# The second sequence's scan: GpSimd adds the two states of every second step, and the planner counts one sum product there

## The chip, the cores and the metric

The kernel runs on one core of a Trainium2 chip. The core has TensorE (PE in the profile; PEld is its weight load), VectorE (DVE), ScalarE (ACT), GpSimd (POOL) and SyncE (SP), which here only issues transfers. The metric is device time in microseconds. Three runs of the kernel before gave 990.7, 991.05 and 991.42 us; the median is 991.05.

## The reference, cut to what matters

The kernel computes a small network of four layers over two sequences (`b` = 0, 1) of 512 positions and 512 features, each with a normalized residual:

```python
x = x + ln(mamba(ln(x)))       # L0_attn: 1024 channels, 16 states a channel
x = x + ln(gptq_ffn(ln(x)))    # L0_ffn: 4-bit weights, 512 -> 1376 -> 512
x = x + ln(attention(ln(x)))   # L1_attn
x = x + ln(latent_moe(ln(x)))  # L1_ffn
```

The change is in the first layer, a selective scan. For every channel d, with 16 states n:

```python
def step(state, inp):                       # over the 512 positions
    dt_t, B_t, C_t, u_t = inp
    dA = exp(dt_t[..., None] * A)
    state = state * dA + (dt_t * u_t)[..., None] * B_t[:, None, :]
    y = einsum('bdn,bn->bd', state, C_t)    # the sum over the 16 states
    return state, y
y = y + u * D
y = y * silu(gate)
out = y @ W_out.T
```

The second layer unpacks 4-bit weights for gate, up and down, and computes `(gate * sigmoid(gate) * up) @ Wd`.

## The kernel before, in words

Everything is float32 with 128 rows (partitions) by 512 columns as the usual tile. In the scan a tile holds 128 channels by 512 positions; a sequence has 8 such channel blocks (`NCH`), so there are 16 blocks in the list `order`: first the 8 of sequence 0, then the 8 of sequence 1. The 16 states of a block are worked two at a time (`NG` = 2), so a block takes 8 steps (`NGI` = 8) and the whole scan 128 (`s` = 0 to 127). Step s belongs to block k = s // 8 and is its step gi = s % 8. Blocks of sequence 1 are steps 64 to 127.

What one step does, engine by engine:

- ScalarE writes exp(dt * A) for the two states into PSUM (`exps`, L970).
- VectorE multiplies `du` (dt times u, in PSUM) by the two rows of B into a `bx` tile of 128 x 2 x 512 (`times_B`, L986), then runs the recurrence over it in place (`scan`, L990). `bx` has six buffers (L625).
- GpSimd multiplies the tile by C in place (`times_C`, L996).
- TensorE adds the states up: `sums` (L998 to L1010) multiplies each of the two halves with the identity and accumulates in the PSUM tile `y`, which has one bank. The block's first sum has one more product in front of it, with the diagonal of D (L1004). A float32 product of 128 x 512 stands in the profile as two records.
- When a block's 16 states are in, `fin` (L1012, its instruction is L1015) multiplies `y` into the gate on VectorE.

A Python loop over s (from L1031 on) writes the instructions out in order, and `pin()` fixes that order for TensorE, ScalarE, VectorE and GpSimd; SyncE's queue is not pinned. Within an iteration s stand: `fin` of the block before (at gi == 2), TensorE's part, `times_B(s + 1)`, `scan(s)`, `exps(s + 2)`, `times_C(s)`. TensorE's part has two halves: the sums of step s - 2, and a stream of other work, `stream()` (L928). A budget decides how much of the stream goes into a step: every step adds `STEP` = 3.5 us, every product takes `MM` = 0.86 us off (L677, L678), sums included, and the stream is drawn from while the budget is above zero. At gi == 2 the stream stands ahead of the sums, else behind them.

The stream is a chain of generators: gates and input products of both sequences, then the output products of sequence 0 (`out_tiles`, L876, with weights `wo` through L834; it waits for `fin` of block 7), the transposes of its normalized rows, and last `ffn0()` (L910): 11 column groups, each with four `fg` and four `fu` products (L919). Each product group spawns a job, run by `tick()` twice an iteration: for a gate, three ScalarE instructions (L656 to L658) and a GpSimd product (L660, `it<-ti,it`); for an up, a VectorE product from PSUM (`ffn_up_job`, L907, `it<-it,fu`). `out_job` copies or reads an output row tile, normalizes it with statistics on VectorE (L119 to L125), small GpSimd instructions (L127, L134), an application on ScalarE (L150), and a GpSimd add into x (L827). Two PSUM banks serve the whole stream, handed from one group to the next in turn (`bank`, `release`).

What the stream hasn't given when the loop ends is written out behind it (`for _ in pe`) and isn't pinned. Then comes stage p3: 32 output products of sequence 1 (`po`, L1092, weights `wo`), the unpacking of the down weights (`once`, L296: loads through L189, L212 and L220, nibbles L226, subtraction L309 on VectorE, product L310 on GpSimd, stores to memory L317 and L327), and 44 down products of sequence 0 (`fo`, L1114, whose weights `wd` are read back through L1109). Its tiles lie where the scan's `bx` tiles lay. The weight tiles `wg`, `wu`, `wo` and `wd` share three buffers of 512 KB (tag `w4`).

Of the kernel before, what the change touches and what calls it, by code (L numbers as in the profile page):

```python
# [29 lines left out]
N_ST = 16  # L30
# [4 lines left out]
NG = 2  # L35
NGI = N_ST // NG
# [20 lines left out]
def tile_sandwich(  # L57
# [5 lines left out]
    nc = tc.nc  # L63
# [24 lines left out]
    ident = const.tile([P, P], F32, name="ident")  # L88
# [299 lines left out]
    def pin():  # L388

        seen = nc.cur_bb.bb.instructions  # L390
        for ins in seen[behind.get("n", 0) :]:
            if ins.engine not in ORDERED:
                continue
            prev = behind.get(ins.engine)
            if prev is not None:
                tc.add_manual_dep(
                    ins, prev.name,
                    mybir.DependencyInfo(mybir.DependencyClass.NoSync, mybir.DependencyReason.DATA),
                    reason="order of tracing",
                )  # L400
            behind[ins.engine] = ins
        behind["n"] = len(seen)
# [6 lines left out]
    with ExitStack() as mamba:  # L409
# [35 lines left out]
        st = {}  # L445
# [21 lines left out]
        def diag(k):  # L467

            c = k % NCH
            t_ = dgp.tile([P, P], F32, tag="dg", name=f"dg{k}")  # L470
            nc.scalar.activation(t_, ident, AF.Copy, scale=ch[:, c, KCONV + 1 : KCONV + 2])
            st["diag", k] = t_
# [49 lines left out]
        def states(b, gi):  # L522

            for lst, lo, nm in ((Bbs[b], 0, "B"), (Cbs[b], R_C - R_B, "C")):
                t_ = bcp.tile([P, NG, S], F32, tag=f"{nm}{gi}", name=f"{nm}{b}_{gi}")
                n0 = lo + gi * NG
                ins = nc.sync.dma_start(
                    out=t_, in_=scr[b][n0 : n0 + NG, :].partition_broadcast(P)
                )
                lst[gi] = t_  # L530
            return ins

        def dt_in(b, c):
            ps = mbank(f"pv{b}_{c}")
            nc.tensor.matmul(ps, wdt[:, ts(c, P)], dtT[b], start=True, stop=True)
            return ps
# [9 lines left out]
        with ExitStack() as p1:  # L546
# [65 lines left out]
            for gi in range(NGI):  # L612
                last = states(0, gi)
# [10 lines left out]
        with ExitStack() as p2:  # L624
# [17 lines left out]
            def spawn(gen, lag=0):  # L642
                jobs.append([now[0] + lag, gen])

            def tick():
                now[0] += 1
                for job in list(jobs):
                    if job[0] <= now[0]:
                        try:
                            job[0] = now[0] + next(job[1])  # L650
                        except StopIteration:
                            jobs.remove(job)
# [12 lines left out]
            def bank_free():  # L665
                return len(turns) < 2 or turns[-2][1] is not None
# [10 lines left out]
            MM = 0.86  # L677
# [283 lines left out]
            order = [(b, c) for b in range(B) for c in range(NCH)]  # L961
            NS = len(order) * NGI
            bxs = {}

            def exps(s):
                k, gi = divmod(s, NGI)
                b, c = order[k]
                for i in range(NG):
                    n = gi * NG + i
                    nc.scalar.activation(  # L970
                        das[s % 2][:, i, 1:], st["dt", b, c][:, 1:], AF.Exp, scale=A[:, c, n : n + 1]
                    )

            def new_du(k):

                b, c = order[k]
                du = st["du"] = ps_du.tile([P, S], F32, tag="du", name=f"du{b}_{c}")
                nc.scalar.copy(du, st["dt", b, c])

            def times_B(s):  # L980
                k, gi = divmod(s, NGI)
                b, c = order[k]
                if gi == 0:
                    nc.vector.tensor_mul(st["du"], u[b][c], st["du"])
                bx = bxs[s] = bxp.tile([P, NG, S], F32, tag="bx", name=f"bx{b}_{c}_{gi}")
                nc.vector.tensor_mul(bx, st["du"].unsqueeze(1).to_broadcast([P, NG, S]), Bbs[b][gi])  # L986

            def scan(s):
                flat = bxs[s].rearrange("p n t -> p (n t)")
                nc.vector.tensor_tensor_scan(  # L990
                    flat, das[s % 2].rearrange("p n t -> p (n t)"), flat, 0.0, ALU.mult, ALU.add
                )

            def times_C(s):
                b, c = order[s // NGI]
                nc.gpsimd.tensor_mul(bxs[s], bxs[s], Cbs[b][s % NGI])  # L996

            def sums(s):  # L998
                k, gi = divmod(s, NGI)
                b, c = order[k]  # L1000
                cost = NG * MM
                if gi == 0:
                    y = st["y"] = ps_y.tile([P, S], F32, tag="y", name=f"py{b}_{c}")
                    nc.tensor.matmul(y, st["diag", k], u[b][c], start=True, stop=False)  # L1004
                    cost += MM
                bx = bxs.pop(s)
                for i in range(NG):
                    n = gi * NG + i
                    nc.tensor.matmul(st["y"], ident, bx[:, i, :], start=False, stop=(n == N_ST - 1))  # L1009
                return cost  # L1010

            def fin(k):  # L1012

                b, c = order[k]
                nc.vector.tensor_mul(g[b][c], g[b][c], st["y"])  # L1015
                st[f"fin{k}"] = now[0]

            def dt_job(k, ps):
                dt_out(*order[k], ps)
                release(f"pv{k}")  # L1020
                yield 1
# [9 lines left out]
            for s in range(NS + 3):  # L1031
                k, gi = divmod(s, NGI)
                free = min(free, MM) + STEP
                if gi == 1 and k + 1 < len(order):
                    dt_due = k + 1
                if gi == 2 and k:
                    fin(k - 1)
                for part in ((1, 0) if gi == 2 else (0, 1)):
                    if part == 0:
                        if 0 <= s - 2 < NS:  # L1040
                            free -= sums(s - 2)
                    else:
                        while free > 0 and s < NS:
                            if dt_due and bank_free():
                                turns.append([f"pv{dt_due}", None])
                                spawn(dt_job(dt_due, dt_in(*order[dt_due])), 2)
                                free -= MM
                                dt_due = None
                            cost = next(pe, None)
                            if cost is None:  # L1050
                                break
                            free -= cost
                tick()
                if gi == 4 and k + 1 < len(order):
                    diag(k + 1)
                if 0 < s < NS - 1:
                    times_B(s + 1)
                    if gi == NGI - 2 and k + 1 < len(order):
                        new_du(k + 1)
                tick()  # L1060
                if s < NS:
                    scan(s)
                    if s == 0:
                        times_B(1)
                    if s + 2 < NS:
                        exps(s + 2)
                    times_C(s)
                    if order[k] == (0, NCH - 1):
                        states(1, gi)
                pin()  # L1070
# [6 lines left out]
        with ExitStack() as p3:  # L1077
# [9 lines left out]
            for j in range(NCH // 2):  # L1087
                w = wo_pair(1, 0, j)
                for e in range(2):
                    c = 2 * j + e  # L1090
                    for i in range(TB):
                        nc.tensor.matmul(  # L1092
                            po[i], g[1][c][:, ts(i, P)], w[:, e, :],
                            start=(c == 0), stop=(c == NCH - 1),
# [9 lines left out]
            for i, m in enumerate(IC):  # L1104
                j, e = divmod(i, 2)
                if not e:
                    w = wst.tile([P, 2, H], F32, tag="w4", name=f"wd0_{j}")
                    n = len(IC[i : i + 2])
# [4 lines left out]
                for t in range(TB):  # L1113
                    nc.tensor.matmul(  # L1114
                        fo[t], its[i][:m, ts(t, P)], w[:m, e],
                        start=(i == 0), stop=(i == len(IC) - 1),
# [279 lines left out]
```

## Time and profile before

| what | us |
|---|---|
| median of three runs | 991.05 |
| the profiled execution, its own time | 991.02 |
| its span, first to last instruction | 989.0 |
| busy: PE, DVE, ACT, POOL | 878.8, 688.8, 426.0, 478.3 |
| first and last scan instruction start | 71.0, 596.0 |
| first `po`, first `fo`, last `fo` product start | 619.1, 646.9, 684.3 |

Times inside the profile count from the span's start. In rows of instruction groups stand the line, the engine, the operation, output and inputs, the shapes, the count, then the busy time, the mean of one in nanoseconds, and the idle time of that engine ahead of them with what ended most of it. In the stretch rows the columns are the stretch, its length, the busy time with the number of instructions for PE, PEld, DVE, ACT and POOL, the granted TensorE clock, the share of DMA time and GB/s. In rows of waits stand who waited, for whom, the time in all, how often, and the longest. In the chain stand start, length, and what ran; "issue" is time in which nothing that the profile shows was waited for, and SPq is SyncE's queue issuing a transfer.

### The profile page before, as it was taken

Reading aid. Unit: us, or ns where it says so; the run is one execution under the profiler, and the core shown is the slowest. Engines: PE = TensorE matmul, PEld = TensorE weight load, DVE = VectorE, ACT = ScalarE, POOL = GpSimd, SP = SyncE. Lnnn points to the kernel's source line nnn. Section 1 sums busy time; section 2 is a strip of 40 time slices with the busy share of each in tenths; the row PEclk is TensorE's granted clock in tenths of the full one; section 3 lists DMA queues with packets and bytes.
Section 4 is the critical chain, followed back from the end, with each engine's and each line's share of the span. In section 5 each row is a group of like instructions: output and inputs, shape, how many; then the busy total and the mean of one; then the engine's idle time right before and its main releaser. Section 6 shows DMA issues by size and latency. Waiting matters only on the chain.

```text
span 989.0 us, 7214 instructions
## 1 busy us (share of the span) xinstructions
PE 878.8 (89%) x2216; PEld 393.8 (40%) x2216; DVE 688.8 (70%) x775; ACT 426.0 (43%) x639; POOL 478.3 (48%) x351
## 2 busy tenths in 40 slices
PE   6966868778899989978999999999999998999994
PEld 3532323233353434423443343444544444455442
DVE  4846999999999998999998995553530014715225
ACT  4345645465666754567664642032430013421212
POOL 4645886787777876776766664450000000001002
PEclk9989998799999989999999999999999999999998
DMA  6358110110100673410100112454322231100101
GB/s 195 113 182 350 43 53 15 37 44 28 43 1 24 209 263 112 139 53 0 43 21 22 42 29 73 143 182 136 127 64 64 58 105 54 64 1 32 54 0 42
DMA packets 43608, 80.61 MB, mean 82 GB/s; under 512 B 7822, under 2 KB 20217, under 8 KB 43570
## 3 DMA queue, kind: packets, MB, share of 16 engines
q1 hardware_dynamic: 40786, 72.72, 22.3%
q0 software_dynamic: 2496, 6.92, 1.8%
q10 hardware_dynamic: 288, 0.52, 0.1%
q8 instruction: 17, 0.28, 0.1%
q14 instruction: 21, 0.17, 0.1%
HBM read 68.90 MB, written 11.24 MB: 81 GB/s over the span
## 4 chain that ended last, share of the span: by engine, by line
PE 39%; DVE 31%; issue 12%; POOL 7%; ACT 2%; DMA 2%; SPq 1%; DVEq 0%; POOLq 0%; ACTq 0%
DVE bx L990 11%; DVE bx L986 8%; PE py L1009 6%; PE pup L1261 5%; POOL bx L996 4%; PE fo L1114 4%; PE pd L1324 4%; PE fu L354 3%; PE fo L1177 3%; PE fg L354 3%; DVE q_gu L226 3%; PE fu L919 2%; PE fg L919 2%; DVE u L462 1%; PE pr L1292 1%
## 5 line engine op out<-in xcount | busy, mean ns | idle before, releaser
L996 POOL TENSOR_TENSOR bx<-bx,C 128x1024 f32<-128x1024 f32 x128 | 301.9, 2360 | 142.2 <-DVE bx L990 131.0
L1009 PE MATMUL py<-bx,ident 128*128 128x512 f32 x512 | 257.2, 633 | 57.6 <-POOL bx L996 57.4
L990 DVE TENSOR_TENSOR_SCAN bx<-da,bx 128x1024 f32<-128x1024 f32 x128 | 291.4, 2277 | 0.1
L970 ACT ACTIVATE da<-dt,A 128x511 f32<-128x511 f32 x256 | 176.6, 691 | 182.3 <-DVE bx L990 177.6
L1009 PEld LDWEIGHTS py<-bx,ident 128*128 128x128 f32 x512 | 98.5, 200 | 195.1 <-issue 97.2
L986 DVE TENSOR_TENSOR bx<-du,B 128x1024 f32<-128x1024 f32 x128 | 154.1, 1204 | 6.4 <-DMA B<-scr 3.4
L1190 DVE TENSOR_TENSOR it<-it,fu 128x512 f32<-128x512 f32 (+1 forms) x11 | 7.6, 687 | 74.0 <-PE fu L354 74.0
L1261 PE MATMUL pup<-hT_l,wup 128*128 128x512 f32 x128 | 57.3, 602 | 0.0
L682 PE MATMUL pg<-xT,w_g 128*128 128x512 f32 x120 | 56.4, 596 | 0.0
L1324 PE MATMUL pd<-wdn,hid 128*128 128x512 f32 x128 | 56.4, 602 | 0.0
L368 POOL TENSOR_TENSOR sd<-ve,half 128x4 f16<-128x4 f16 x2 | 2.1, 1044 | 110.8 <-DVE ve L366 110.8
L462 DVE SCALAR_TENSOR_TENSOR u<-px,ch,u 128x511 f32<-128x511 f32 (+2 forms) x48 | 35.8, 746 | 14.5 <-ACT u L455 13.4
L127 POOL TENSOR_TENSOR rs_lo<-ve_lo,mhalf 128x1 f32<-128x1 f32 x8 | 6.0, 744 | 78.0 <-DVE ve_lo L125 75.2
L919 PE MATMUL fu<-hT_f,wu 128*128 128x512 f32 (+1 forms) x88 | 41.5, 593 | 0.7 <-ACT dt L540 0.7
L919 PE MATMUL fg<-hT_f,wg 128*128 128x512 f32 (+1 forms) x88 | 41.6, 594 | 0.0
L354 PE MATMUL fg<-hT_f,wg 128*128 128x512 f32 (+1 forms) x88 | 40.2, 593 | 0.7 <-ACT hT_f L171 0.7
L354 PE MATMUL fu<-hT_f,wu 128*128 128x512 f32 (+1 forms) x88 | 40.6, 603 | 0.0
L1177 PE MATMUL fo<-wd,it 128*128 128x512 f32 (+1 forms) x88 | 40.0, 598 | 0.0
L226 DVE TENSOR_SCALAR q_gu<-qw_gu 128x512 int32<-128x512 int32 (+1 forms) x24 | 34.3, 1428 | 7.1 <-DMA qw_gu<-in_up_q 7.1
L1114 PE MATMUL fo<-wd,it 128*128 128x512 f32 (+1 forms) x88 | 38.0, 593 | 0.2 <-DMA wd<-wd_d 0.2
L1324 PEld LDWEIGHTS pd<-wdn,hid 128*128 128x128 f32 x128 | 24.9, 194 | 31.8 <-issue 31.2
L1261 PEld LDWEIGHTS pup<-hT_l,wup 128*128 128x128 f32 x128 | 24.5, 195 | 28.8 <-issue 28.8
(224 smaller groups left out, 1142.6 us busy)
## 6 DMA issues: line engine op xcount, KB each, us to landing
wo<-in_W_outT SPq DMA_DIRECT2D x20, 512.0 KB
B<-scr SPq DMA_DIRECT2D x16, 512.0 KB
C<-scr SPq DMA_DIRECT2D x16, 512.0 KB
wg<-wgu_d SPq DMA_DIRECT2D x10, 512.0 KB
wu<-wgu_d SPq DMA_DIRECT2D x10, 512.0 KB
w_x<-in_W_in SPq DMA_DIRECT2D x8, 512.0 KB
wgu_d<-w_gu POOLq DMA_DIRECT2D x16, 256.0 KB, 2.3
w_g<-in_W_in SPq DMA_DIRECT2D x8, 512.0 KB
```

Of the source, the lines that this page charges most:

```text
L226: nc.vector.tensor_scalar(q, qw, 4 * j, 15, ALU.logical_shift_right, ALU.bitwise_and)
L354: nc.tensor.matmul(ps[:m], w[:, kc, e * P : e * P + m], hT[:, kc, :], start=(kc == 0), stop=(kc == KH - 1),)
L919: nc.tensor.matmul(ps[:m], wt[j][a][:, kc, e * P : e * P + m], hT[:, kc, :], start=(kc == 0), stop=(kc == KH - 1),)
L970: nc.scalar.activation(das[s % 2][:, i, 1:], st["dt", b, c][:, 1:], AF.Exp, scale=A[:, c, n : n + 1])
L986: nc.vector.tensor_mul(bx, st["du"].unsqueeze(1).to_broadcast([P, NG, S]), Bbs[b][gi])
L990: nc.vector.tensor_tensor_scan(flat, das[s % 2].rearrange("p n t -> p (n t)"), flat, 0.0, ALU.mult, ALU.add)
L996: nc.gpsimd.tensor_mul(bxs[s], bxs[s], Cbs[b][s % NGI])
L1009: nc.tensor.matmul(st["y"], ident, bx[:, i, :], start=False, stop=(n == N_ST - 1))
L1114: nc.tensor.matmul(fo[t], its[i][:m, ts(t, P)], w[:m, e], start=(i == 0), stop=(i == len(IC) - 1),)
L1177: nc.tensor.matmul(fo[t], its[i][:m, ts(t, P)], w[:m], start=(i == 0), stop=(i == len(IC) - 1),)
L1261: nc.tensor.matmul(ps, w[:, kc, ts(e, P)], src[kc], start=(kc == 0), stop=(kc == KH - 1))
L1324: nc.tensor.matmul(pd, hid[kc][:, ts(i, P)], wdn[kc], start=(kc == 0), stop=(kc == INT // P - 1),)
```

## The change

In sequence 1, every step with odd s is "paired": behind the product by C, GpSimd also adds the second half of the `bx` tile to the first, and TensorE sums only the first half. So 4 of a block's 8 steps have one sum product in place of two, and the planner's budget is charged one product less there. In the iterations that hold the sums of a paired step, the stream is written ahead of the sums, as it was already at gi == 2. The budget left goes to the stream, so gate and up of sequence 0 are drawn earlier. Nothing of the result is left out; only the order of the additions differs.

```diff
             def times_C(s):
                 b, c = order[s // NGI]
                 nc.gpsimd.tensor_mul(bxs[s], bxs[s], Cbs[b][s % NGI])
+                if paired(s):
+                    nc.gpsimd.tensor_add(bxs[s][:, 0, :], bxs[s][:, 0, :], bxs[s][:, 1, :])
+
+            def paired(s):
+
+                return order[s // NGI][0] == 1 and s % 2 == 1
 
             def sums(s):
                 k, gi = divmod(s, NGI)
                 b, c = order[k]
-                cost = NG * MM
+                ns = 1 if paired(s) else NG
+                cost = ns * MM
...
                 bx = bxs.pop(s)
-                for i in range(NG):
-                    n = gi * NG + i
-                    nc.tensor.matmul(st["y"], ident, bx[:, i, :], start=False, stop=(n == N_ST - 1))
+                for i in range(ns):
+                    last = gi == NGI - 1 and i == ns - 1
+                    nc.tensor.matmul(st["y"], ident, bx[:, i, :], start=False, stop=last)
                 return cost
...
-                for part in ((1, 0) if gi == 2 else (0, 1)):
+                for part in ((1, 0) if gi == 2 or 2 <= s < NS + 2 and paired(s - 2) else (0, 1)):
```

## The prediction

> **What bounds the kernel now.** I read the page's costliest groups, then busy time by stretches that I cut at the channels of the second sequence's scan (eight steps each) and at the stages behind it, then the waits of VectorE in that scan, last the chain from the scan's end on. First the groups of the scan, from the page:
>
> ```profile
> L996 POOL TENSOR_TENSOR bx<-bx,C 128x1024 f32<-128x1024 f32 x128 | 301.9, 2360 | 142.2 <-DVE bx L990 131.0
> L1009 PE MATMUL py<-bx,ident 128*128 128x512 f32 x512 | 257.2, 633 | 57.6 <-POOL bx L996 57.4
> L990 DVE TENSOR_TENSOR_SCAN bx<-da,bx 128x1024 f32<-128x1024 f32 x128 | 291.4, 2277 | 0.1
> L986 DVE TENSOR_TENSOR bx<-du,B 128x1024 f32<-128x1024 f32 x128 | 154.1, 1204 | 6.4 <-DMA B<-scr 3.4
> ```
>
> A step costs VectorE 2.28 + 1.20 us; scans with nothing else between them start 3.31 us apart, because neighbours overlap a little. Each of the 256 sums stands as two records 0.43 us apart, so one product holds TensorE 0.86 us. Busy time by stretch (stretch, length, PE, PEld, DVE, ACT, POOL, granted clock, DMA share, GB/s):
>
> ```profile
> 354.60:386.50 31.90, 28.28 (x58) 11.67 (x57) 28.93 (x22) 15.47 (x22) 19.65 (x10) 0.89 0.54 185
> 386.50:418.20 31.70, 31.70 (x74) 13.69 (x73) 31.43 (x28) 20.01 (x28) 24.53 (x15) 1.00 0.40 133
> 507.40:539.70 32.30, 31.02 (x72) 13.20 (x71) 29.71 (x21) 18.62 (x29) 21.99 (x11) 1.00 0.12 33
> 569.50:598.20 28.70, 27.12 (x63) 11.61 (x62) 27.37 (x19) 11.20 (x17) 20.85 (x10) 1.00 0.09 26
> 598.20:618.70 20.50, 20.29 (x48) 8.27 (x47) 9.36 (x22) 4.80 (x9) 8.82 (x7) 1.00 0.29 90
> 618.70:646.90 28.20, 28.04 (x67) 12.15 (x65) 15.07 (x23) 1.76 (x3) 12.85 (x13) 1.00 0.45 152
> ```
>
> Inside the scan VectorE is the bound (idle 0.1 to 3 us a channel, some 10 us in all), with TensorE just below it. Behind the scan TensorE is full and VectorE half empty. What VectorE waited for from 355 to 600 us:
>
> ```profile
> DVE it L907 <- PE fu L919: 5.8, 4, 2.5
> DVE bx L986 <- issue: 1.2, 1, 1.2
> DVE du L984 <- ACT du L978: 0.9, 1, 0.9
> DVE st_mo L119 <- ACT o L840: 0.7, 1, 0.7
> DVE st_f L119 <- POOL x L827: 0.4, 1, 0.4
> ```
>
> The chain from the scan's end, shortened, and two waits of SyncE's queue between 595 and 650 us:
>
> ```profile
> 602.93 2.58 PE fu L919 x6
> 605.51 3.45 PE fg L919 x8
> 608.97 0.38 SPq L111
> 609.40 3.07 DMA z_d<-zd_d
> ...
> 613.17 0.68 DVE it L907
> ...
> 621.53 2.37 issue
> 623.90 0.67 DVE it L907
> ...
> 627.33 2.60 POOL w_d L310 x2
> ```
> ```profile
> SPq L111 <- PE fg L919: 1.3, 1, 1.3
> SPq L1109 <- PE po L1092: 0.4, 1, 0.4
> ```
>
> Two strands run from the scan's end to the first `fo` product at 646.87: TensorE's own (19 left-over gate and up products from 602.3 to 618.65, then 32 `po` products, 27.5 us), and the down weights (`zw_d` load at 600.82, unpacking, `wd` load issued at 642.88 and landed at 646.8). They end within 0.2 us of each other. The gate and up rest lies in both: its `wu` load stands in SyncE's queue ahead of the `z_d` load, and its `it` products sit between the unpacking instructions.
>
> **Part 1, TensorE's sums.** 32 of the second sequence's 128 sum products go: 32 x 0.86 = 27.5 us. The planner gives 3.5 us a step, 28 a channel, or 32.6 products. Sums, diagonal and dt took 18 of them; now 14. The stream of other products rises from 14.6 to 18.6 a channel. Working its rules through, gate and up now start at step 89 (before: 92) and take 88 products: 88 / 18.6 x 8 = 38 steps, so the last falls at about step 125 of 127. Nothing is left behind the scan: 19 x 0.86 = 16.3 us leave that strand.
>
> **Part 2, GpSimd's adds.** The nearest rows are GpSimd's own two-input 128x512 products, `it<-ti,it` and `x<-x,o`, 1.27 us each (1.71 once, beside VectorE's unpacking). 32 x 1.27 = 40.6 us, 5.1 a channel, against 7.2 us idle in the tightest channel (31.7 - 24.5) and 12.3 in the loosest. So on the sum it fits under VectorE; if it did not, GpSimd at 29.6 of 31.7 us would pace that channel. What gets late is the odd step's sum. VectorE's instructions of the step do not slow beside GpSimd: scans took 2256 to 2290 ns throughout. The Trainium skill, GPSIMD Engine Reference, section 4.1, speaks against the change: two-input elementwise work belongs on VectorE, GpSimd being about half as fast. The rows agree on the speed (0.68 us for VectorE's `it` product, 1.27 here); by the rule the 32 adds would cost 21.8 us on the engine that is the bound, by the rows they cost nothing where GpSimd is idle, so I go by the rows.
>
> **Part 3, the scan on VectorE (its end at 598.2).**
> - Three `it` products move into the scan: 3 x 0.68 = +2.0.
> - Waits of `it` for `fu` (5.8 us): in most odd steps the stream now runs ahead of the sums, and by the plan all but one `fu` group ends early in its step; one wait of about 1 us stays: -4.8.
> - First channel: the first output row tile's last product stands a step earlier, so the 0.7 and 0.9 us behind its copy go: -1.6. The 1.2 us for a `bx` buffer stays (TensorE waits for the first `wo` load as before).
> - `fin` now comes behind a stream block. In the first channel I add up TensorE's list from 372.83 (end of sum 64): 15 stream products, one dt and 10 sum products, 26 by 0.86, bring the last sum to 395.2 (before 392.6), where VectorE arrives at 391.6; 0.9 us of the wait is filled with a norm that the faster stream moves ahead: +2.6. In the other channels the last sum ends about 8.4 us after its scan began (even sum, five products, one sum), and VectorE needs it 8.8 after: no wait to 2 us each, taken as +1.8 together.
> - `x` adds of GpSimd that now queue behind a state add, with VectorE's statistics behind them: three times 0 to 1.3, taken as +1.0.
> Sum: +1.0. Ends: -5.4 (no new wait, all old ones gone) to +7 (`fin` waits a product or more in every channel).
>
> **Part 4, behind the scan.** The `zw_d` load waited for a sum of step 126, an even one: unchanged against the scan's end. The last sum itself ends 0.4 later (add +1.27, one product less). Then: VectorE's unpacking of the zeros loses a 1.43 us wait and a 0.69 us product between its parts, and the `z_d` load no longer stands behind `wu`: -2.0. In the eight words the interval is 2.02 us where nothing interferes and 3.02 and 2.77 about GpSimd's and VectorE's `it`: -1.8. The `wo` loads, whose buffers came free with the gate and up weights, move ahead of all this: -0.4. The unpacking ends about 4 us earlier, and TensorE's `po` ends at 630.6 instead of 646.7. When `fo` starts is then up to where the `wd` load stands in SyncE's queue. Before, it waited for a buffer that `po` gave back, now free 16 us earlier. Behind the first six stores of the second part, as before: 646.9 - 3.9 (gain 3.9). Directly behind that part's loads: issue 633.5 + 3.95 = 637.5 (gain 9.4). Directly behind the first part's stores: 632.6 (gain 14.3). TensorE's own limit is 16.3. I take the middle, 9.4, since the wait that held the load was the buffer.
> TensorE then idles near 7 us ahead of `fo`. At 357.7 to 363.3 it idled as long, and the granted clock was 0.5 in two slices of 3.4 us: up to 3.4 us lost, 1.7 taken. The Trainium skill, TensorE: Matmul & The Clock Gate, in its closing table, warns of gaps over about 3 us; by it the whole 3.4 us of half clock would be paid and the gain would be 0 to 1.7 us smaller than mine.
> So -7.7 here. All that follows hangs on `fo`'s end (the chain goes on through its copies and statistics into attention) and moves with it.
>
> **Sum.** +1.0 - 7.7 = -6.7. The profiled span 989.0 becomes 982.3; with the 2.0 us around it (991.02 - 989.0) that is 984.3. The median before, 991.05, is that same run within 0.03.
>
> **Rivals.**
> - *Hidden anyway* (15%): the `wd` load keeps its place behind the stores, and TensorE only idles. 989.0 + 1.0 - 3.9 + 2 = 988.1. For it: the two strands end together now. Against: the buffer wait named above.
> - *Slower* (17%): `fin`, first in line on VectorE with the next step's products and scan behind it, waits for the odd sum behind GpSimd's add and a full stream block. From 8 waits that grow by 1.7 us (two products) over my +1.0 the loss of 13.6 us passes the gain of 6.7; time about 998 at worst, 993 to 998. For it: TensorE has 0 to 1.3 us idle in several channels, and the planner fills what is freed. Against: 3.5 us of plan a step, while VectorE's real steps average 3.73 (scans of steps 88 and 108 start at 450.90 and 525.57).
> - *All of it* (10%): `wd` goes out directly behind the first stores and the scan gets shorter: 989 - 4 - 13 + 2 = 974.
> - *No change that can be told* (2%): the waits just cancel.
> My forecast keeps 56%, with its own range 979 to 989.
>
> **Numbers.** 0.2% is 2 us, about what can be told from no change. Slower than 993: the slower rival, 0.17. Within 2 us: 0.06 (edges of the hidden and of the slower case). Faster: 0.77. The range leaves out half of "all of it" (5%) and the worse three quarters of the slower case (13%): 973.5 to 994.5.
>
> **What would show it.** No L919 product behind the scan, and `po` directly after the last sum; GpSimd at 85 to 95% in the second sequence's channels with adds of 1.27 us; the wait "it for fu" near 1 us; a new wait "g for py" of some 4 us in all, the largest near 392; an idle TensorE of 2 to 10 us ahead of the first `fo`. Wrong if the scan ends later than 605, if the adds take over 1.5 us, or if `fo` starts no earlier than 645.

## The result, and the profile after

Twelve runs of the changed kernel gave a median of 989.43 us (986.77 to 994.07), twelve of the kernel before on the same chip 991.23 (987.98 to 993.41). The ratio is 0.9991, with a 95% interval of 0.9971 to 1.0012: no change that can be told. The changed kernel's times fall into two groups, 986.8 to 989.6 (seven) and 992.9 to 994.1 (five), and the profiled execution, 986.77 us with a span of 985.0, is of the lower one.

Both profiles cut into the same stages, in us, each length worked out from the starts and ends of the instructions named:

| stage | before | changed |
|---|---|---|
| up to the start of scan 64 | 355.8 | 357.4 |
| second half of the scan: start of scan 64 to end of scan 127 | 242.5 | 248.1 |
| gap: end of scan 127 to the first `fo` product | 48.6 | 38.5 |
| `fo`: first to last product of the stage | 38.0 | 40.2 |
| last stage: from there to the end | 304.1 | 300.8 |

So 10.1 us were won in the gap, 2.2 given back in `fo`, and 5.6 in the scan. The first and the last row hold the same code in both kernels and differ by +1.6 and -3.3. A half-clock slice is a stretch in which the granted TensorE clock was 0.5; up to TensorE's last product the last stage had 14 us of them before and 7 in the changed kernel, and the difference is worth up to 3.4 us. So the clock can account for the 3.3 us; that the change brings them about isn't shown. First the scan's groups on the page of the changed kernel:

```profile
L996 POOL TENSOR_TENSOR bx<-bx,C 128x1024 f32<-128x1024 f32 x128 | 301.8, 2359 | 107.3 <-DVE bx L990 93.9
L1016 PE MATMUL py<-bx,ident 128*128 128x512 f32 x448 | 234.1, 650 | 64.8 <-POOL bx L996 55.5
L998 POOL TENSOR_TENSOR bx<-bx 128x512 f32<-128x512 f32 x32 | 40.5, 1267 | 2.5
```

The change did what it says: 64 records, 32 products, fewer in the sums (now L1016), and 32 adds of 1.27 us on GpSimd (L998). Busy time by stretch in the changed kernel, two channels of the scan, the gap and `fo`, with the columns as before:

```profile
388.50:422.20 33.70, 29.41 (x68) 12.32 (x67) 29.93 (x31) 20.69 (x29) 27.37 (x22) 0.97 0.46 148
576.10:605.50 29.40, 25.03 (x55) 9.98 (x54) 27.54 (x19) 12.71 (x20) 26.22 (x14) 0.93 0.18 60
605.50:640.60 35.10, 33.41 (x70) 13.64 (x68) 16.00 (x28) 1.76 (x3) 14.61 (x10) 0.91 0.28 96
640.60:684.00 43.40, 38.24 (x89) 16.69 (x89) 18.41 (x52) 9.13 (x11) 16.15 (x24) 1.00 0.44 137
```

GpSimd is at 81 to 89% of these channels and not the bound. VectorE is idle 3.8 us in the first row and 1.9 in the second, where it had 0.3 and 1.3 before. What it waited for in the second half of the scan:

```profile
DVE g L1022 <- PE py L1016: 4.2, 2, 3.4
DVE it L907 <- POOL it L660: 3.2, 3, 1.8
DVE it L907 <- PE fu L919: 2.1, 1, 2.1
DVE st_f L119 <- POOL x L827: 1.9, 2, 1.5
DVE bx L986 <- POOL bx L998: 1.1, 1, 1.1
```

The second line is new: the up product waits for GpSimd's gate product, which waits in GpSimd's queue behind a state add. Its largest case, in GpSimd's instructions in order of time and then VectorE's:

```profile
597.64 2.36 POOL L996 TENSOR_TENSOR bx<-bx,C 128x1024 f32<-128x1024 f32 x1 [0.60 <-DVE bx L990]
600.08 1.26 POOL L998 TENSOR_TENSOR bx<-bx 128x512 f32<-128x512 f32 x1
601.29 1.27 POOL L660 TENSOR_TENSOR it<-ti,it 96x512 f32<-96x512 f32 x1
602.52 2.35 POOL L996 TENSOR_TENSOR bx<-bx,C 128x1024 f32<-128x1024 f32 x1
```
```profile
602.59 0.68 DVE L907 TENSOR_TENSOR it<-it,fu 96x512 f32<-96x512 f32 x1 [1.79 <-POOL it L660]
603.20 2.28 DVE L990 TENSOR_TENSOR_SCAN bx<-da,bx 128x1024 f32<-128x1024 f32 x1
```

The last scan stands behind `it` in VectorE's queue and starts 1.8 us late for it. Behind the scan, SyncE's queue and TensorE in order of time:

```profile
583.65 13.33 SPq L834 DMA_DIRECT2D wo<-in_W_outT  x3
608.57 0.32 SPq L189 DMA_DIRECT2D zw_d<-in_down_z  x1
...
638.07 2.17 SPq L220 DMA_DIRECT2D z_d<-zd_d  x3
640.35 0.95 SPq L1116 DMA_DIRECT2D wd<-wd_d  x2
```
```profile
611.31 29.40 PE L1099 MATMUL po<-wo,g 128*128 128x512 f32 x64 [0.82 <-issue]
643.97 20.87 PE L1121 MATMUL fo<-wd,it 128*128 128x512 f32 x48 [3.26 <-DMA wd<-wd_d]
666.73 17.43 PE L1121 MATMUL fo<-wd,it 128*128 128x512 f32 x40 [1.89 <-DMA wd<-wd_d]
```

No gate or up product is left; three `wo` loads went out while the scan still ran; `po` follows the last sum within 1 us; the `wd` load (now L1116) stands directly behind the `z_d` loads, and TensorE idles 3.3 us until it has landed. It waits a second time inside `fo`, 1.9 us for a later `wd` load, where the kernel before waited 0.2 us in all: that is most of `fo`'s 2.2 us, and the granted clock was 1.00 there.

### The profile page after: what moved, and what is told of

It is laid out like the page before. It is cut to its first block, busy times and chain, and to the rows that moved or that the text cites. A ratio compares the mean times of both kernels' runs of the same rounds, so it can differ in the third digit from the quotient of the medians.

```text
span 985.0 us, 7131 instructions
## 1 busy us (share of the span) xinstructions
PE 857.0 (87%) x2152; PEld 381.9 (39%) x2152; DVE 688.2 (70%) x775; ACT 426.0 (43%) x639; POOL 517.6 (53%) x383
## 4 chain that ended last, share of the span: by engine, by line
PE 36%; DVE 31%; issue 12%; POOL 8%; DMA 4%; ACT 2%; SPq 1%; DVEq 0%; POOLq 0%; ACTq 0%
DVE bx L990 12%; DVE bx L986 9%; PE pd L1331 6%; PE pup L1268 5%; POOL bx L996 3%; PE fu L354 3%; PE fo L1184 3%; PE fg L354 3%; PE py L1016 3%; DVE q_gu L226 3%; PE po L888 2%; DMA C<-scr 2%; PE fo L1121 2%; DVE u L462 1%; PE pr L1299 1%
## 5 line engine op out<-in xcount | busy, mean ns | idle before, releaser
L1016 PE MATMUL py<-bx,ident 128*128 128x512 f32 x448 | 234.1, 650 | 64.8 <-POOL bx L996 55.5
L1016 PEld LDWEIGHTS py<-bx,ident 128*128 128x128 f32 x448 | 87.5, 205 | 193.0 <-POOL bx L996 91.7
L998 POOL TENSOR_TENSOR bx<-bx 128x512 f32<-128x512 f32 x32 | 40.5, 1267 | 2.5
L354 PE MATMUL fg<-hT_f,wg 128*128 128x512 f32 (+1 forms) x88 | 40.2, 593 | 0.7 <-ACT hT_f L171 0.7
L354 PE MATMUL fu<-hT_f,wu 128*128 128x512 f32 (+1 forms) x88 | 39.8, 593 | 0.0
L1184 PE MATMUL fo<-wd,it 128*128 128x512 f32 (+1 forms) x88 | 39.6, 592 | 0.0
```

Source lines behind the costliest of these rows:

```text
L354: nc.tensor.matmul(ps[:m], w[:, kc, e * P : e * P + m], hT[:, kc, :], start=(kc == 0), stop=(kc == KH - 1),)
L1184: nc.tensor.matmul(fo[t], its[i][:m, ts(t, P)], w[:m], start=(i == 0), stop=(i == len(IC) - 1),)
```

## The experiments

Two theories for the 5.6 us of the scan. G: GpSimd's longer queue makes VectorE wait. P: the fuller plan and the stream ahead of the sums do. The table has the stages of each kernel's profiled execution (half of the scan, gap, `fo`, last stage), the half clock in the scan's half and in the last stage up to TensorE's last product, all in us, and the times against the kernel before on the same chip.

| kernel | half | gap | fo | last | half clock | median | ratio, 95% interval |
|---|---|---|---|---|---|---|---|
| before | 242.5 | 48.6 | 38.0 | 304.1 | 14, 14 | 991.2 | 1 |
| changed | 248.1 | 38.5 | 40.2 | 300.8 | 31, 7 | 989.4 | 0.9991 (0.9971 to 1.0012) |
| changed again | 248.1 | 38.7 | 40.1 | 300.8 | 28, 7 | 993.4 | 0.9995 (0.9970 to 1.0020) |
| adds only | 244.7 | 49.1 | 38.0 | 305.8 | 24, 20 | 995.1 | 1.0025 (1.0007 to 1.0043) |
| sums first | 249.1 | 39.6 | 40.1 | 300.8 | 24, 7 | 987.5 | 0.9960 (0.9946 to 0.9974) |
| no adds | 246.9 | 36.1 | 40.2 | 304.1 | 27, 14 | 987.2 | 0.9956 (0.9940 to 0.9972) |
| plan only | 254.6 | 36.4 | 39.7 | 302.5 | 10, 10 | 991.5 | 1.0004 (0.9988 to 1.0019) |
| pairs from 72 | 245.8 | 40.4 | 41.0 | 300.8 | 29, 7 | 985.8 | 0.9939 (0.9923 to 0.9955) |
| pairs from 88 | 244.7 | 39.0 | 39.8 | 302.1 | 24, 14 | 983.5 | 0.9926 (0.9912 to 0.9939) |
| adds behind jobs | 240.9 | 40.4 | 39.7 | 305.5 | 14, 20 | 984.4 | 0.9918 (0.9900 to 0.9937) |

The half clock alone doesn't order the halves: plan only has the least of it (10 us) and the longest half.

### Adds only

```diff
-                cost = ns * MM
+                cost = NG * MM
...
-                for part in ((1, 0) if gi == 2 or 2 <= s < NS + 2 and paired(s - 2) else (0, 1)):
+                for part in ((1, 0) if gi == 2 else (0, 1)):
```

> The 32 adds and the 32 missing sum products alone: the planner is charged as before and the sums stand ahead of the stream as before, so 19 gate and up products stay behind the scan. The second sequence's half of the scan (start of scan 64 to end of scan 127) took 242.5 us before and 248.1 in the changed kernel. Theory G (GpSimd's longer queue lengthens the scan: VectorE waits for the it product, the x add and a bx buffer behind state adds): the half stays at 245 to 248, waits of VectorE for GpSimd 3 us or more. Theory P (the fuller plan and the stream ahead of the sums lengthen it): 240 to 242.5, no wait of fin for the sum over 1 us. Both: the gap from the scan's end to the first fo product stays near 48.6, total within 3 us of before under P, 2 to 6 slower under G.

The half took 244.7, between the two; the gap stayed at 49.1. VectorE's waits in the half:

```profile
DVE it L907 <- PE fu L919: 6.9, 5, 1.9
DVE st_f L119 <- POOL x L827: 1.8, 1, 1.8
DVE bx L986 <- POOL bx L998: 1.5, 1, 1.5
DVE it L907 <- POOL it L660: 0.7, 1, 0.7
```

4.0 us of waits for GpSimd, as G has it, and none of `fin`, as P has it. The adds alone lengthen the half by 2.2 us and win nothing: what the change gains, it gains only by the products that leave the gap. The kernel is 0.25% slower, but not all of that is the adds': its ten times run from 988.0 to 996.6, and the profiled one lost 1.7 us in the last stage, which had 20 us of half clock for 14.

### Sums first

```diff
-                for part in ((1, 0) if gi == 2 or 2 <= s < NS + 2 and paired(s - 2) else (0, 1)):
+                for part in ((1, 0) if gi == 2 else (0, 1)):
```

> The changed kernel with the sums ahead of the stream again in odd steps; adds and the lower charge stay. Theory P: the 3.4 us wait of fin in the first channel shrinks by 2 to 3.4, waits of it for fu grow by up to 2, half of the scan 245 to 247. Theory G: the half stays at 247 to 249, since GpSimd's queue is the same. Both: gap behind the scan 38 to 40 us, total within 3 us of the changed kernel.

The wait of `fin` fell to 0.5, but the half stayed long, 249.1: waits of `it` for `fu` rose to 4.2, and a 3.3 us wait of `du` for ScalarE is new. The order of the two parts moves the waits and doesn't decide the length of the half; P falls as far as it meant the order. The waits for GpSimd stay (2.5 of `it`, 1.4 of the statistics behind an x add, 0.9 of `bx`), as G has it. The four times lie between 986.1 and 988.2.

### No adds

```diff
                 nc.gpsimd.tensor_mul(bxs[s], bxs[s], Cbs[b][s % NGI])
-                if paired(s):
-                    nc.gpsimd.tensor_add(bxs[s][:, 0, :], bxs[s][:, 0, :], bxs[s][:, 1, :])
```

> The changed kernel without the 32 adds, so the second state of every odd step of sequence 1 is left out of the sum; plan and order as changed. Theory G: half of the scan falls from 248.1 to 242 to 244, no wait of VectorE for GpSimd over 1 us. Theory P: it stays at 246 to 249, fin's wait of 3.4 us with it. Gap behind the scan 38 to 39 under both.

246.9, outside G's 242 to 244 and inside P's 246 to 249. Its waits:

```profile
DVE g L1020 <- PE py L1014: 4.8, 2, 3.4
DVE it L907 <- PE fu L919: 4.7, 2, 3.3
```

The wait of 3.4 us of `fin` stays, as P has it: it comes from the plan and the order, not from the adds. The waits for GpSimd are nearly gone (0.4 and 0.5 left), as G has it, and longer ones of `it` for TensorE stand in their place. But this execution had a half-clock slice of 6.8 us at 487.4, which the changed kernel's first profile has not; the last experiment below shows one at 491.7 with the same two waits of `it`, 1.95 and 3.29 us against 0.1 and 2.07 without it. This kernel has 1.46 and 3.29 there. Taking 1.4 and 1.2 off leaves an estimate of 244.3 without the slice: by it the adds account for some 4 of the 5.6 us, and the rest is the three `it` products (2.0). That this kernel would run without the slice is not shown: TensorE waited 3.05 us in one piece across the slice's start, where the changed kernel waits 1.69. So this run alone doesn't settle what the adds cost.

### Plan only

```diff
-                if paired(s):
-                    nc.gpsimd.tensor_add(bxs[s][:, 0, :], bxs[s][:, 0, :], bxs[s][:, 1, :])
...
-                ns = 1 if paired(s) else NG
-                cost = ns * MM
+                ns = NG
+                cost = (1 if paired(s) else NG) * MM
```

> The changed kernel's plan and order with both sum products kept and no adds: TensorE gets the 19 gate and up products into the scan without being relieved. Without the adds but with one product less, the half of the scan took 246.9 us (242.5 before). If the relief of TensorE is what makes room: 32 products more, 27.5 us, into a stretch where TensorE had about 20 us idle, so the half grows to 255 or more, gap behind the scan about 37, total 3 to 10 us slower than before. If the room was there anyway: half 247 to 250, total like the changed kernel's.

```profile
DVE g L1020 <- PE py L1014: 9.8, 5, 5.8
DVE it L907 <- PE fu L919: 5.7, 2, 4.5
```

The half grew to 254.6, close to the first reading's 255, and the gap fell to 36.4, so the total stayed at 1.0004 and didn't lose the 3 to 10 us that were expected with it. Moving the products without relief costs the scan about what it saves behind it. The relief is worth 6.5 us of the half (254.6 against 248.1), net of what the adds cost there.

### Pairs from step 88, and from step 72

```diff
-                return order[s // NGI][0] == 1 and s % 2 == 1
+                return s >= 11 * NGI and s % 2 == 1
```

> Pairs only from step 88 on: 20 adds. By the planner's rules 1 gate and up product is left behind the scan, the output products of sequence 0 keep their places of before. Both theories lose what sits in steps 64 to 87 (fin 3.4, x adds 1.5): half of the scan 243 to 245, gap behind it 39 to 41, so 4 to 6 us less than the changed kernel's profile and 984 to 986 in time. Theory G: the it products still wait some 3 us for GpSimd. Theory P: they don't.

```profile
DVE bx L986 <- issue: 2.5, 1, 2.5
DVE it L907 <- PE fu L919: 2.4, 1, 2.4
DVE it L907 <- POOL it L660: 2.1, 3, 0.7
DVE g L1022 <- PE py L1016: 0.8, 1, 0.8
```

Half 244.7, gap 39.0, and 983.5 us, 0.74% faster than before, the five times between 983.3 and 985.9. The 12 adds of steps 64 to 87 had bought one product behind the scan, not more. As G says, `it` still waits for GpSimd.

With `s >= 9 * NGI` in that line (pairs from 72):

> Pairs from step 72 on, so the first channel of sequence 1 (steps 64 to 71), where TensorE is behind by 10 us after waiting for the first output weights, keeps its old plan. If the fuller plan of that channel is what makes fin wait (3.4 us): that wait falls under 1, half of the scan 245 to 246. If the output products of any channel do it: the wait moves to the next fin, half 247 to 248. All 19 products stay inside the scan, gap behind it 38 to 39.

The 3.4 us wait of `fin` at step 74 is gone, the half 245.8, but a wait of 1.8 for GpSimd's x add came at step 85 and one of 1.6 of `fin` at step 106. So what made `fin` wait at step 74 sits in the first channel, where TensorE is 10 us late (GpSimd's product of step 64 ends at 362.3 in the changed kernel, its sums start at 372.7). It is the full plan together with the stream ahead of the sums: with the full plan and the sums first, that wait was 0.5. The gap was 40.4 where 38 to 39 was expected, with 13 us of half clock in it (6 in the changed kernel). In time, 985.8.

### The add behind the jobs

From the kernel with pairs from 88:

```diff
-                if paired(s):
-                    nc.gpsimd.tensor_add(bxs[s][:, 0, :], bxs[s][:, 0, :], bxs[s][:, 1, :])
+            def add_states(s):
+                nc.gpsimd.tensor_add(bxs[s][:, 0, :], bxs[s][:, 0, :], bxs[s][:, 1, :])
...
                 tick()
+                if 0 < s <= NS and paired(s - 1):
+                    add_states(s - 1)
                 if s < NS:
                     scan(s)
```

> Pairs from step 88 on, and each state add is written behind the jobs of the next iteration, so GpSimd's it product goes ahead of it. If the it products wait because they queue behind adds: the 2.1 us of waits of it for GpSimd fall under 0.5, half of the scan 242 to 244 (244.7 with the adds in front), total 0 to 2 us under that kernel's 983.5. If the sums then come too late: a wait of fin or of it for TensorE grows by as much and nothing is won.

```profile
DVE it L907 <- PE fu L919: 2.4, 1, 2.4
DVE bx L986 <- issue: 1.3, 1, 1.3
DVE g L1023 <- PE py L1017: 0.7, 1, 0.7
```

No wait of `it` for GpSimd is left, and `fin` waits no longer than before. The half is 240.9, 3.8 us shorter and below the 242.5 of the kernel before, though it holds more work. Of the 3.8 us, 2.1 are these waits. Another 1.2 are the `bx` wait, which is chance: it falls at step 69, ahead of the first pair, where both kernels hold the same code, and the kernel with pairs from 88 had a 6.8 us half-clock slice at 362.9 there and waited 3.0 us for `wo` instead of 1.4. The gap is 1.4 longer. In time, 984.4, it can't be told from the kernel with pairs from 88; both are faster than the kernel before and, by the intervals in the table, than the changed kernel.

### The changed kernel again

> The changed kernel once more, to see its spread beside the others on one chip and whether the stages of its first profile repeat: half of the scan 247 to 249, gap behind it 38 to 39, fo stage 40, wait of fin in the first channel 3 to 4 us. If the time is two-valued (987 and 993 in the first runs), the length of the last stage (fo's end to the end, 300.8 us with 7 us of half clock in the first profile) differs by the half-clock slices in it.

The stages repeat within 0.2 us (248.1, 38.7, 40.1, 300.8) and so do VectorE's five waits within 0.1. Twelve times: five from 983.7 to 989.6, seven from 993.1 to 995.7. The profiled execution, 985.4, is again of the lower group, so four more profiles of the same kernel followed, one execution each:

> The changed kernel, one look. Its 24 times so far fall into 983.7 to 989.6 and 992.9 to 995.7, both profiles are of the lower group. Theory C (clock): an execution of the upper group has 20 to 35 us more half clock, and the stages where TensorE is the bound behind the scan (from the first po product to the end) are longer by 5 to 8 us, the half of the scan by under 2. Theory S (scan): the half of the scan itself is 5 us or more longer, with more waits of VectorE, and the rest is as in the first profiles (po to fo 33, fo 40, last stage 300.8).

> As the look before: if the time is of the upper group, C puts the difference behind the scan in half-clock slices, S into the scan. If of the lower group, the stages repeat: half of the scan 248.1, gap 38.5, fo 40, last stage 301.

(The second passage was the expectation for the second, third and fourth profile.) Three were of the lower group (987.7, 985.5, 985.3), with a half of 248.1 to 248.2. The fourth took 995.08: half 253.0, gap 40.4, `fo` 40.7, last stage 302.5. So it is S by place, 4.8 of the 9.6 us over the second profile in the scan's half, and C by cause, as the clock shows. The second part of the half and then the gap, by stretch, first in the second profile (lower group), then in the fourth:

```profile
484.00:604.00 120.00, 109.70 (x246) 45.35 (x246) 114.31 (x79) 67.56 (x103) 105.37 (x57) 0.98 0.13 39
604.00:642.80 38.80, 33.59 (x70) 13.64 (x68) 17.55 (x34) 1.76 (x3) 16.06 (x12) 0.92 0.32 108
```
```profile
486.70:609.60 122.90, 111.68 (x246) 46.28 (x245) 114.19 (x78) 67.34 (x103) 105.14 (x57) 0.96 0.13 38
609.60:650.00 40.40, 35.49 (x70) 14.18 (x68) 18.34 (x34) 1.75 (x3) 16.06 (x12) 0.84 0.31 103
```

VectorE and GpSimd did the same work; the granted clock was lower. TensorE around step 97, second profile and fourth:

```profile
486.94 1.13 PE L1016 MATMUL py<-bx,ident 128*128 128x512 f32 x2 [0.62 <-POOL bx L998]
489.76 3.70 PE L919 MATMUL fu<-hT_f,wu 128*128 128x512 f32 x8 [1.69 <-ACT dt L540]
```
```profile
489.48 1.12 PE L1016 MATMUL py<-bx,ident 128*128 128x512 f32 x2 [0.62 <-POOL bx L998]
492.30 6.77 PE L919 MATMUL fu<-hT_f,wu 128*128 128x512 f32 x8 [1.70 <-ACT dt L540]
```

The same order, the same waits, and eight `fu` records take 6.77 instead of 3.70 us, since the clock was at half from 491.7 to 498.5. VectorE's `it` then waits 1.95 us at step 99 and 3.29 at step 105. A longer slice at 450.7 (6.8 us against 3.4) slows TensorE's sums and transposes there, and `fin` waits 1.8 longer at step 90. Together the waits grow by 4.9 us, and the half by 4.8. This is shown for one execution of the upper group; that the other twelve are alike is argued from their mean clocks, 0.938 to 0.945 against 0.943 to 0.956 in the lower group, which overlap.

## Why the prediction was right or wrong

Forecast 984.3, with 77% for faster; measured no change that can be told. The time lies inside the range, the direction wasn't borne out. The sign named for "wrong", a scan that ends later than 605, came: it ended at 605.5.

- **What stands.** Product count, add price (1.27), `po` straight behind the last sum, and the gap: -9.4 forecast, -10.1 measured, with the `wd` load just where the middle case put it, directly behind the second part's loads. The last gate and up product fell in step 125 (its last record starts at 596.0), as named, though the sum beside it, 38 steps from step 89 on, ends at 127.
- **Right by luck behind the scan.** The 1.7 us of lost clock in `fo` rested on a misreading: from 357.7 to 363.3 in the profile before it was the `wo` load that took that long, while TensorE was busy for 4.24 of the 5.60 us and waited 2.2 us ahead of it and 1.4 at its end. In the first profile of the changed kernel `fo` had no half clock at all. It took 2.2 us longer for a second wait for a `wd` load, 1.9 us, which the forecast didn't have. The idle ahead of `fo` was 3.3 us and not 7, and the half clock fell on `po` (29.4 for 27.5), whose end `fo` wasn't waiting for. So -7.7 forecast and -8.0 measured agree in part by chance.
- **`fin`.** +2.6 and +1.8 forecast; 3.4 at step 74 and 0.8 at step 90, 4.2 in all. The last sum of the first channel ended at 397.1; less the 1.6 us by which this half began later, that is 395.5, against 395.2 as added up.
- **The x adds.** +1.0 forecast, +1.5 measured (1.9 against 0.4).
- **The step that failed: "one wait of about 1 us stays: -4.8".** The waits of `it` came to 5.3 us (3.2 for GpSimd, 2.1 for TensorE) against 5.8, so -0.5, which is 4.3 of the 4.6 us that the scan's sum is off. I asked only when `fu` was ready on TensorE. `it` has a second input, GpSimd's gate product, and a state add ahead of it in GpSimd's queue delays that by 1.3 us. I had drawn just this conclusion for the x adds and not for the product next to them. The add behind the jobs shows it: with the gate product first, that wait is nil. The 2.1 us for TensorE are a second, smaller miss in the same term. With -0.5 in it the forecast's whole sum is -2.4 in place of -6.7, about the 2 us that it called the edge of no change.
- **The scan's sum.** +2.0 (three products) - 0.5 - 1.6 (both first-channel waits went) + 4.2 + 1.5 - 0.1 (`bx`) = +5.5; measured +5.6, forecast +1.0.
- **What the sum left out.** Half clock inside the scan. The lower group (983.7 to 989.6) lies around the forecast or up to 5 us over it, and the first profile is that near in part because the two stages whose code is the same came out at -3.3 and +1.6. In the upper group the 9.6 us of the fourth profile come on top. I had priced the clock at one place behind the scan, and not where TensorE's waits would bring it between the steps.
- **The rivals.** "Hidden anyway" fell: the gap shrank by 10.1. "Slower" had the right place, VectorE's queue head, with the wrong head: `fin` waited 4.2 us and not 13.6; `it` was the other half. The outcome given 6%, within 2 us of the kernel before, is the one that came: the medians lie 1.8 us apart.

## What to carry to other kernels

When an instruction is added to an engine that has time to spare, list every instruction behind it in that queue and ask who waits for each, not only for the result of the added one; here the adds fitted into GpSimd's idle time and still left VectorE some 4 us of waits for GpSimd (4.0 in adds only). With 20 adds, writing them behind the small jobs took away the 2.1 us that `it` still waited. Put such relief only where it buys something: 20 of the 32 adds won nearly all that 32 did in the gap (39.0 against 38.5) and saved the waits of the others. Where TensorE runs close to the bound engine, the clock alone can set two executions of one kernel 9.6 us apart, and one profile then says little of the median.

## What the runs showed of the hardware that I had not expected

The half-clock slices start on a grid: in the second of the four profiles at 357.6, 364.4, 419.0, 425.8 and 449.7, which are 2, 16, 2 and 7 times 3.41 us apart, and they last 3.4, 6.8 or 10.2. Whether one falls on a given stretch differs between executions of the same program with the same waits (at 491.7 in the fourth, none there in the other five profiles of the changed kernel). One thing that differed is how the work lay against the grid: counted from the start of scan 96, the next grid point stood at 1.7 us in the fourth and at 3.1 to 3.2 in the other five (slice starts less scan starts, by whole multiples of 3.41). The longest single wait of TensorE from 463 us up to the products that the slice hit was 1.70 us, with two of about 0.6 just before it. The Trainium skill, TensorE: Matmul & The Clock Gate, closing table, warns of gaps over about 3 us; here shorter ones were enough, and the measurement decides. The same page, Part 1, describes a free-running window over which activity is judged; the grid agrees with that, and so does a slice that comes or not as the waits lie against it, though no run here moved the grid on purpose.
